# An AdaLN block with sliding-window attention and a mixture of experts: the setup issued in a written order, weight splits on VectorE, and the slot buffer blanked from the load queue

## Chip, cores and metric

The kernel runs on one core of a Trainium2 chip. The metric is the device time of one execution in microseconds, as the median of several runs. A profile is one execution with the hardware profiler on.

## What is computed

Two sequences of 2048 tokens with 256 features go through one block: attention with a window of 128 and 16 heads of 64, then a top-2 mixture of 8 experts with a capacity of 640 rows per expert and choice. Both halves are modulated by rows that come from a small conditioning vector `c` (2 x 256). All is float32. Cut to what matters:

```python
mod = (silu(c) @ wmod).reshape(2, 6, 1, 256)
sa, ca, ga, sb, cb, gb = (mod[:, i] for i in range(6))
ga = sign(ga) * maximum(abs(ga), 0.25)           # gb alike
h = layernorm(x) * (1 + ca) + sa
q, k, v = split(h @ Wqkv)                        # Wqkv 256 x 3072
x = x + ga * (softmax(window(q @ k.T / 8)) @ v) @ Wout   # Wout 1024 x 256
h = layernorm(x) * (1 + cb) + sb
# top-2 of 8 experts per token, 640 rows per expert and choice, later tokens dropped
y = sum over the two choices of prob * (relu(rows @ W1[e] + b1[e]) @ W2[e] + b2[e])
out = x + gb * y
```

## The kernel before

**Precision.** A float32 operand of a large product is split in two parts of type fp32r: the higher, `hi`, is a copy or a scaled copy by ScalarE (ACT), and the lower, `lo`, is the operand less `hi`, by VectorE (DVE) or, for some weights, by GpSimd (POOL). `passes` (L227) makes each product of three matmuls, hi by hi, hi by lo and lo by hi. `split` (L124) splits a loaded weight, `part` (L298) a projection in PSUM.

**Work of the attention.** The 4096 tokens are 16 groups `g` of 256 (two tiles of 128). The 16 heads are 8 pairs. An iteration `w` (L1084) covers two pairs of one group, so there are four iterations to a group, and it works on four stages at once: `new` = the pairs of w (scores, `pack`, `maximum`, first exponentials), `old` = those of w-1 (rest of the exponentials, `normalize`), `turned` = those of w-2 (`turn`, `unpack`, `values`), `done` = those of w-3 (`out_project`). Projections of q and k for iteration w+1 and of v for the group run in the same iteration. `pack` (L510) copies scores from PSUM to SBUF with the window's mask, on ACT (L526) and DVE (L519 for the first group of a sequence, L527). `out_project` uses `wo[:, :, hp, :]`, so pairs 0 to 3 need the first half of Wout (from iteration 3 on) and pairs 4 to 7 the second (from iteration 5 on).

**Order of work.** The attention's iterations stand under `manual_schedule`: each engine runs its instructions in the order in which the program writes them, and so does the queue that SyncE (SP) issues. The setup before it (L322 to L1155) isn't: there a planner orders each engine's instructions by its own estimate. Side work is placed in the iterations by hand: `place` (L1039) puts a generator's steps at given places, such as "1A" (one iteration on, place A), and `go` (L1077) takes one step of each generator that is due at (w, place). `NORM` (L1030) has the places for a group's layer norm, `norm` (L240).

**PSUM.** Six banks are a ring (`bank`, L91) for scores, turned tiles, projections and values; a tile's bank comes free once its reader on ACT or DVE is done.

**Setup.** `norm(0)` makes the first group's normalized rows. The weights of q, k and v come in six pieces of 512 KB (L399 to L407), each loaded by SP to a "raw" buffer and split; the raw buffers are two in the pool `stage` and two in the pool `sp`, taken by turns. POOL does the lower part of three of these pieces and of the second half of Wout. Wout comes in two halves (L409 to L416). The modulation's first two parts are needed as columns (`cols`, L378 to L394), the other four as rows: four rows are made by PE and DVE at L433 to L453 (`wide4`), stored to DRAM (`rowd`, L454) and loaded back broadcast over the partitions (`load_rows`, L116, and `gbr`, L457). `x` is loaded by groups (`load_x`, L203) to three buffers.

**Blanking the slots.** The experts' rows are collected in DRAM in `xbuf`, 10240 rows of 274 floats. Before the first rows are scattered there, each row gets zeros and an invalid token number. The rows' source is the tile `blank`, one row in each partition, in a "raw" buffer of `stage` (L461). `clear(i)` (L465) writes the 1280 rows of an expert with two transfers, each with the row of a partition repeated five times. ACT's queue issues them, four in each of the iterations 1 to 4 (L1088 to L1090).

Of the kernel before, what the change touches and what calls it, by code (L numbers as in the profile page):

```python
# [8 lines left out]
FP = mybir.dt.float32  # L9
FR = mybir.dt.float32r  # L10
I32 = mybir.dt.int32
AF = mybir.ActivationFunctionType
ALU = mybir.AluOpType
# [15 lines left out]
def adaln_block_kernel(  # L29
# [61 lines left out]
    def bank(name, shape=(P, 512)):  # L91
        return ring["pool"].tile(list(shape), FP, tag="ring", name=name, bufs=ring["bufs"])
# [38 lines left out]
            nc.scalar.mul(hi, raw, scale)  # L131
            nc.vector.scalar_tensor_tensor(lo, raw, scale, hi, ALU.mult, ALU.subtract)

    def load(src, shape, name, pool=stage):
        raw = pool.tile(shape, FP, tag="raw", name=f"raw_{name}", bufs=2)
        nc.sync.dma_start(out=raw, in_=src)
        return raw

    def load_split(hi, lo, src, shape, name, scale=None, pool=stage, eng=nc.vector):
        split(hi, lo, load(src, shape, name, pool), scale, eng)  # L140

    class Expert:

# [96 lines left out]
    def norm(g):  # L240

        b = g // GPB
        xg = xs[g]
        mv, rs = norm_stats(xg, f"a{g}")
        yield
        z = wk.tile([P, SBT, D], FP, tag="t2", name=f"z_{g}")
        for t in range(SBT):
            nc.vector.tensor_scalar(
                z[:, t, :], xg[:, t, :], mv[:, t, 0:1], rs[:, t : t + 1],
                ALU.subtract, ALU.mult,  # L250
            )
        yield
        tp = bank(f"tp_h{g}")
        for k in range(ND):
            for t in range(SBT):
                nc.tensor.transpose(
                    tp[:, k * TS + t * P : k * TS + (t + 1) * P], z[:, t, k * P : (k + 1) * P], ident
                )
        hT = wk.tile([P, ND, TS], FP, tag="t2", name=f"hT_{g}")
        for k in range(ND):  # L260
            nc.vector.tensor_scalar(
                hT[:, k, :], tp[:, k * TS : (k + 1) * TS],
                cols[:, 1, k, b : b + 1], cols[:, 0, k, b : b + 1], ALU.mult, ALU.add,
            )
        yield
        hh = wk.tile([P, ND, TS], FR, tag="hh", name=f"hh_{g}")
        hl = wk.tile([P, ND, TS], FR, tag="hl", name=f"hl_{g}")
        nc.scalar.copy(hh, hT)  # L268
        yield
        nc.vector.tensor_tensor(hl, hT, hh, ALU.subtract)  # L270
        hs[g] = (hh, hl)
        yield
# [25 lines left out]
    def part(dh, dl, src):  # L298
        nc.scalar.copy(dh, src)
        nc.vector.tensor_tensor(dl, src, dh, ALU.subtract)  # L300
# [18 lines left out]
        vs[g, t, hf] = v  # L319


    first = norm(0)  # L322
    with tc.tile_pool(name="setup", bufs=1) as sp:
        cr = sp.tile([B * ND, P], FP, name="cr")
# [2 lines left out]
        wm = sp.tile([P, ND, 6 * D], FP, name="wm")  # L327
        wmv = wmod.rearrange("(k p) f -> p k f", p=P)
        nc.sync.dma_start(out=wm[:, :, 0 : 2 * D], in_=wmv[:, :, 0 : 2 * D])
        gw = sp.tile([E, D], FP, name="gw")  # L330
        nc.scalar.dma_start(out=gw, in_=gate_w)
        b1r = sp.tile([E * NF, P], FP, name="b1r")
        nc.scalar.dma_start(out=b1r, in_=b1.rearrange("e (k p) -> (e k) p", p=P))
        nc.scalar.dma_start(
            out=gbias, in_=gate_b.rearrange("(a e) -> a e", a=1).to_broadcast([P, E])
        )
        make_identity(nc, ident)

        nc.gpsimd.memset(ones, 1.0)
# [26 lines left out]
        next(first)  # L366


        sg = sp.tile([B * ND, P], FP, name="sg")
        nc.scalar.activation(sg, cr, AF.Exp, scale=-1.0)  # L370
        nc.vector.tensor_scalar(sg, sg, 1.0, None, ALU.add)
        nc.vector.reciprocal(sg, sg)
        nc.vector.tensor_tensor(sg, sg, cr, ALU.mult)
        tp = bank("tp_c")
        nc.tensor.transpose(tp[:, 0 : B * ND], sg, ident[0 : B * ND, 0 : B * ND])
        scT = sp.tile([P, B, ND], FP, name="scT")
        nc.vector.tensor_copy(scT.rearrange("p b k -> p (b k)"), tp[:, 0 : B * ND])
        mc = bank("mod_cols")  # L378
        for m in range(2):
            for d in range(ND):  # L380
                o = (m * ND + d) * B
                for k in range(ND):
                    nc.tensor.matmul(
                        out=mc[:, o : o + B],
                        lhsT=wm[:, k, m * D + d * P : m * D + (d + 1) * P],
                        rhs=scT[:, :, k],
                        start=(k == 0),
                        stop=(k == ND - 1),
                    )
        colf = cols.rearrange("p m d b -> p (m d b)")  # L390
        nc.vector.tensor_copy(colf[:, 0 : ND * B], mc[:, 0 : ND * B])
        nc.vector.tensor_scalar(
            colf[:, ND * B : 2 * ND * B], mc[:, ND * B : 2 * ND * B], 1.0, None, ALU.add
        )  # L394

        for _ in first:
            pass

        for i in range(2):  # L399
            for j in range(3):  # L400
                f = slice(j * HD + i * HD // 2, j * HD + (i + 1) * HD // 2)
                load_split(
                    wq[:, 0, :, f], wq[:, 1, :, f], wqkv[:, f].rearrange("(k p) f -> p k f", p=P),
                    [P, ND, HD // 2], f"wq{i}_{j}", QSCALE if j == 0 else None,
                    pool=sp if (3 * i + j) % 2 else stage,
                    eng=nc.gpsimd if j == 1 or (i, j) == (0, 2) else nc.vector,
                )  # L407
        nc.sync.dma_start(out=wm[:, :, 2 * D :], in_=wmv[:, :, 2 * D :])
        for i in range(2):  # L409
            s = slice(i * NP // 2, (i + 1) * NP // 2)  # L410
            load_split(
                wo[:, 0, s, :], wo[:, 1, s, :],
                wout[i * HD // 2 : (i + 1) * HD // 2, :].rearrange("(k p) d -> p k d", p=P),
                [P, NP // 2, D], f"wo{i}", pool=stage if i else sp,
                eng=nc.gpsimd if i else nc.vector,
            )  # L416
        part(*project_qk(0, 0, 0))

        tp = bank("tp_g")
        for k in range(ND):  # L420
            nc.tensor.transpose(
# [3 lines left out]
        tp = bank("tp_b1")  # L425
        nc.tensor.transpose(tp[:, 0 : E * NF], b1r, ident[0 : E * NF, 0 : E * NF])
        nc.vector.tensor_copy(b1T, tp[:, 0 : E * NF])


        wide4 = sp.tile([B, 4, D], FP, name="wide4")  # L430
# [2 lines left out]
        for g in range(2):  # L433
            mr = bank(f"mod_rows{g}")
            for k in range(ND):
                nc.tensor.matmul(
                    out=mr[0:B, :],
                    lhsT=scT[:, :, k],
                    rhs=wm[:, k, (2 + 2 * g) * D : (4 + 2 * g) * D],
                    start=(k == 0),  # L440
                    stop=(k == ND - 1),
                )
            gate, plain = (mr[0:B, 0:D], mr[0:B, D:]) if g == 0 else (mr[0:B, D:], mr[0:B, 0:D])
            nc.vector.tensor_scalar(sgn, gate, 0.0, 2.0, ALU.is_ge, ALU.mult)
            nc.vector.tensor_scalar(sgn, sgn, -1.0, None, ALU.add)
            nc.vector.tensor_tensor(mag, gate, sgn, ALU.mult)
            nc.vector.scalar_tensor_tensor(
                wide4[:, 3 * g, :], mag, 0.25, sgn, ALU.max, ALU.mult
            )
            if g == 0:  # L450
                nc.vector.tensor_copy(wide4[:, 1, :], plain)
            else:
                nc.vector.tensor_scalar(wide4[:, 2, :], plain, 1.0, None, ALU.add)  # L453
        nc.sync.dma_start(out=rowd, in_=wide4)  # L454
        load_rows(0)
        for b in range(B):
            nc.sync.dma_start(out=gbr[:, b, :], in_=rowd[b, 3:4, :].to_broadcast([P, D]))  # L457


        xs[1] = load_x(1)  # L460
        blank = stage.tile([P, ROW], FP, tag="raw", name="blank")  # L461
        nc.gpsimd.memset(blank, 0.0)
        nc.gpsimd.memset(blank[:, TOK : TOK + 1].bitcast(I32), 2 * T)

    def clear(i):  # L465

        for r0 in range(i * BUF, (i + 1) * BUF, CAP):
            nc.scalar.dma_start(
                out=xbuf[r0 : r0 + CAP, :].rearrange("(p n) d -> p n d", p=P),
                in_=blank.rearrange("p (a d) -> p a d", a=1).to_broadcast([P, CAP // P, ROW]),  # L470
            )


    wl = attn.enter_context(tc.tile_pool(name="work_late", bufs=2, reuse_waits="tile"))
# [552 lines left out]
    VALUES = [[(0, 0)], [(1, 0)], [(0, 1)], [(1, 1)]]  # L1027
    LAST_VALUES = [[(0, 0), (1, 0)], [(0, 1)], [], []]

    NORM = ["0B", "1A", "1H", "2A", "2B"]  # L1030
    CLOSE = ["0H", "1A", "1B", "2H", "3H", "4A", "4B", "5H", "6A", "6B", "6C"]
    LATE = {
        NG - 3: ["0H", "1A", "1B", "2B", "2H", "3A", "3B", "3H", "3C", "3C", "3C"],
# [49 lines left out]

    def iteration(w):  # L1084
        g, p2 = divmod(w, NP // 2)
        if p2 == NP // 2 - 1 and g + 2 < NG:
            xs[g + 2] = load_x(g + 2)
        for i in range(2 * w - 2, 2 * w):  # L1088
            if 0 <= i < E:
                clear(i)  # L1090
        new, old, turned, done = pair(w), pair(w - 1), pair(w - 2), pair(w - 3)

        ahead = [divmod(i, NP // 2) for i in range(w + 1, NW if w == NW - 3 else w + 2) if i < NW]
# [58 lines left out]
            exps(*new[0], [2, 3])  # L1152
        go(w, "V")

    part(*project_qk(0, 0, 1))  # L1155
    everything = {mybir.EngineType.PE, mybir.EngineType.Activation, mybir.EngineType.DVE, mybir.EngineType.Pool, mybir.EngineType.SP}
    order = tc.manual_schedule(engines=everything)
    order.__enter__()
    for w in range(NW + 3):
        iteration(w)  # L1160

# [135 lines left out]
```

## Time and profile before

| | us |
|---|---|
| median of 3 runs | 1161.58 (1160.19 to 1163.09) |
| the profiled execution | 1161.56 |
| its span, first to last instruction | 1159.8 |

| engine | busy us | share of the span |
|---|---|---|
| PE (matmul) | 1086.3 | 94% |
| PEld (weight load, beside PE) | 999.6 | 86% |
| DVE | 877.4 | 76% |
| ACT | 676.7 | 58% |
| POOL | 593.8 | 51% |

The span's first 30 us or so are the setup, with PE busy 6 tenths of the first slice of 29 us; the attention follows to about 760 us, then the experts. The granted clock of PE is 0.97 on average, with spells of 0.50.

How to read it: a row of a time line has the start, the duration, the engine, the line of the kernel, the operation, what it writes and reads, and in brackets the idle time before it with what ended that. "SPq" and "ACTq" are the queues on which SP and ACT issue transfers; the duration there is that of issuing. "To landing" is the time from issue until the data have arrived. A row for a stretch of time has, for each engine, the busy us in it and the count of instructions, then PE's granted clock, the mean busy share of the 16 DMA engines, and GB/s.

### The profile page before, as it was taken

To read this page: it belongs to the slowest core of one execution; us is meant where nothing else is said; L and a number is where in the kernel's file an instruction comes from. 1 tells how busy PE (TensorE), PEld (TensorE's weight loads), DVE (VectorE), ACT (ScalarE), POOL (GpSimd) and SP (SyncE) were. 2 spreads that over 40 slices of the span, in tenths; PEclk is the share of its full clock that TensorE was granted. 3 is DMA by queue.
4 is the path that set the end of the run, shared out by engine and by line. 5 is a ranking of instruction groups with operands and counts; after the bars stand their busy time and mean duration, and the time that the engine had idled before them with its cause. 6 is when DMAs were issued, how large, how long until landed. Compare 5 with 4: busy or idle time off the path is not lost. (4 is left out here: it accounts for less than half of the span.)

```text
span 1159.8 us, 25187 instructions
## 1 busy us (share of the span) xinstructions
PE 1086.3 (94%) x9246; PEld 999.6 (86%) x9246; DVE 877.4 (76%) x2168; ACT 676.7 (58%) x2097; POOL 593.8 (51%) x769
## 2 busy tenths in 40 slices
PE   6799999999999999999999997779889999999995
PEld 4678999999999888999999896768879999999995
DVE  6556688888878778888878877767667777878764
ACT  4467776777777567777777676423344444344441
POOL 4235465665675556665675665433522615443524
PEclk9899999999999999999999998879989999999998
DMA  6890010010010010010010022233432524342413
GB/s 228 194 218 21 1 39 19 21 39 19 21 39 19 21 43 29 21 36 20 17 37 20 18 65 70 85 91 95 83 106 87 84 84 90 83 89 67 83 45 36
DMA packets 59571, 72.09 MB, mean 62 GB/s; under 512 B 4807, under 2 KB 51152, under 8 KB 59436
## 3 DMA queue, kind: packets, MB, share of 16 engines
q1 hardware_dynamic: 36988, 44.27, 12.2%
q0 software_dynamic: 11712, 14.79, 7.4%
q10 hardware_dynamic: 10736, 11.27, 4.3%
q8 instruction: 80, 1.31, 0.5%
q14 instruction: 55, 0.45, 0.1%
HBM read 40.11 MB, written 32.27 MB: 62 GB/s over the span
## 5 line engine op out<-in xcount | busy, mean ns | idle before, releaser
L937 ACT ACTIVATE hm<-ph,b1T 128x256 fp32r<-128x256 f32 (+2 forms) x184 | 99.3, 540 | 224.8 <-PE ph L232 192.6
L232 PE MATMUL pq<-hh,wq 128*128 128x256 f32 x1024 | 216.8, 295 | 3.5 <-ACT hh L268 3.0
L232 PE MATMUL ph<-xT,we 128*128 128x256 f32 (+2 forms) x1104 | 203.6, 325 | 15.5 <-DVE xT L127 4.6
L550 ACT ACTIVATE pm<-pm,mx 128x128 f32<-128x128 f32 x512 | 204.1, 402 | 19.4 <-DVE mx L536 16.7
L232 PE MATMUL y<-we,hm 128*128 128x256 f32 x1440 | 201.5, 285 | 6.6 <-DVE hm L939 6.6
L232 PEld LDWEIGHTS y<-we,hm 128*128 128x128 f32 x1440 | 186.7, 190 | 10.7 <-DVE hm L939 9.3
L232 PEld LDWEIGHTS ph<-xT,we 128*128 128x128 f32 x1104 | 172.3, 196 | 21.2 <-issue 6.5
L584 POOL TENSOR_SCALAR_AFFINE_SELECT pT<-pT 128x512 f32<-128x512 f32 (+1 forms) x128 | 80.9, 632 | 211.6 <-ACT pT L583 211.5
L232 PEld LDWEIGHTS pq<-hh,wq 128*128 128x128 f32 x1024 | 170.0, 193 | 5.8 <-ACT hh L268 3.4
L938 DVE TENSOR_SCALAR r<-ph,b1T 128x256 f32<-128x256 f32 (+2 forms) x184 | 101.8, 562 | 73.1 <-ACT hm L937 65.6
L560 POOL TENSOR_TENSOR pm<-pm,rd 128x512 f32<-128x512 f32 x128 | 133.8, 1045 | 28.5 <-DVE rd L558 26.4
L232 PE MATMUL pq<-hl,wq 128*128 128x256 f32 x512 | 145.8, 285 | 0.0
L526 ACT COPY pm<-sc 128x256 f32<-128x256 f32 (+1 forms) x256 | 80.6, 363 | 107.9 <-PE sc L502 70.3
L1002 POOL TENSOR_TENSOR ys<-ys,gw 128x256 f32<-128x256 f32 x56 | 48.4, 971 | 175.7 <-DVE ys L992 157.0
L607 PE MATMUL av<-pT,v 128*64 128x128 f32 (+1 forms) x1472 | 126.7, 321 | 4.7 <-POOL pT L588 2.2
L607 PEld LDWEIGHTS av<-pT,v 128*64 128x64 f32 x1472 | 91.1, 140 | 33.7 <-POOL pT L588 4.6
L1003 POOL DMA_INDIRECT out_dram<-ys,tok x60 | 98.1, 1634 | 33.5 <-issue 11.4
L527 DVE COPY_PREDICATED pm<-within,sc 128x256 f32<-128x256 int32 (+1 forms) x256 | 96.1, 422 | 22.0 <-ACT pm L526 21.1
L502 PE MATMUL sc<-kr,qh 64*128 64x256 f32 (+1 forms) x1024 | 105.7, 296 | 5.0 <-DVE ql L300 2.0
L550 ACT ACTIVATION_READ_ACCUMULATOR pm<-pm,mx 128x1 f32 x512 | 99.6, 194 | 0.0
L232 PEld LDWEIGHTS pq<-hl,wq 128*128 128x128 f32 x512 | 99.0, 193 | 0.0
L939 DVE TENSOR_TENSOR hm<-r,hm 128x256 fp32r<-128x256 f32 (+2 forms) x144 | 94.6, 657 | 5.3
(162 smaller groups left out, 2261.9 us busy)
## 6 DMA issues: line engine op xcount, KB each, us to landing
raw_w<-in_L_ffn_W_dram SPq DMA_DIRECT2D x32, 512.0 KB, 3.9
xbuf<-blank ACTq DMA_DIRECT2D x16, 685.0 KB, 9.6
xt<-xbuf SPq DMA_DIRECT2D x8, 822.0 KB, 4.9
x<-in_L_attn_x_dram SPq DMA_DIRECT2D x16, 256.0 KB, 2.8
out_dram<-x SPq DMA_DIRECT2D x16, 256.0 KB, 2.3
xt<-xbuf SPq DMA_DIRECT2D x7, 548.0 KB, 5.0
raw_wq<-in_L_attn_Wqkv_dram SPq DMA_DIRECT2D x6, 512.0 KB, 7.0
wm<-in_L_wmod_dram SPq DMA_DIRECT2D x1, 1024.0 KB, 11.1
```

The costliest lines, as they stand in the source:

```text
L232: nc.tensor.matmul(out=out_, lhsT=a, rhs=b, start=start and n == 0 and i == 0, stop=stop and n == last and i == 2, **kw,)
L502: nc.tensor.matmul(out=sc[h][:, t, lo:], lhsT=q[r, t * P : (t + 1) * P], rhs=kr[r, (0, 1, 0)[i], hp, blk, :], start=(i == 0), stop=(i == 2),)
L526: nc.scalar.copy(pm[:, h, ts, :], blocks[:, own, :])
L527: nc.vector.copy_predicated(pm[:, h, ts, :], within.rearrange("p (a k) -> p a k", a=1).to_broadcast([P, n, P]), blocks[:, before, :],)
L550: nc.scalar.activation(pm[:, h, t, :], pm[:, h, t, :], AF.Exp, bias=mx[:, h, t : t + 1], accum_out=den[:, h, t : t + 1],)
L560: nc.gpsimd.tensor_tensor(pmv, pmv, rd.rearrange("p h (t a) -> p (h t) a", a=1).to_broadcast([P, 2 * SBT, P]), ALU.mult,)
L584: nc.gpsimd.affine_select(out=pT[:, :, t0:, 0, :], in_=own[:, :, t0:, :], pattern=[[0, 2], [0, n], [-1, P]], compare_op=ALU.is_gt, fill=0. ...
L607: nc.tensor.matmul(out=av[h * DH : (h + 1) * DH, q0 : q0 + hi - lo], lhsT=v[:, f0 + h * DH : f0 + (h + 1) * DH], rhs=pT[:, h, lo:hi], star ...
L937: nc.scalar.activation(hh[:, s], phv, AF.Relu, bias=bias)
L938: nc.vector.tensor_scalar(r[:, s], phv, bias, 0.0, ALU.add, ALU.max)
L939: nc.vector.tensor_tensor(hl, r[:, 0:W], hh, ALU.subtract)
L1003: add = nc.gpsimd.indirect_dma_start(out=of, out_offset=bass.IndirectOffsetOnAxis(ap=tok[:, 0:1], axis=0), in_=y, in_offset=None, bounds_c ...
```

## The change

- `manual_schedule` is entered ahead of the setup, so that the setup too runs in written order on all five engines. The setup's text is put in another order for it.
- The six weight pieces of q, k and v get five raw buffers in `sp`, and functions of their own: `get(n)` loads, `high(n)` is ACT's part, `low(n)` DVE's. POOL has no lower part any more; `load_split` is gone. Pieces 0 to 2 are loaded ahead of the small loads of `gw`, `b1` and the gate's bias, which move from ACT's queue to SP's; then the rest of `wmod`, `x` of group 1, pieces 3 and 4. Piece 5 is loaded after the first two projections.
- The layer norm has one more step (between the transposes and `hT`); `NORM` has "1H" twice for it.
- `norm(0)`'s steps, the splits, the two first projections, the gate's and bias's transposes and the modulation rows are interleaved by hand. The modulation rows come after both first projections.
- `blank` is filled early. `clear` has no argument: it issues all sixteen transfers, on SP's queue, once, before iteration 0.
- Wout is loaded by a generator, `load_output`: its first step (before the loop) loads the first half, its second (iteration 1, place A) splits that half and loads the second, its third (iteration 1, place C) splits the second.
- `x` of group 2 is loaded before the loop; it stood in iteration 3, and the planner issued it at about 6 us.

```diff
-    def load_split(hi, lo, src, shape, name, scale=None, pool=stage, eng=nc.vector):
-        split(hi, lo, load(src, shape, name, pool), scale, eng)
...
+    everything = {
+        mybir.EngineType.PE, mybir.EngineType.Activation, mybir.EngineType.DVE,
+        mybir.EngineType.Pool, mybir.EngineType.SP,
+    }
+    order = tc.manual_schedule(engines=everything)
+    order.__enter__()
     first = norm(0)
...
+        def get(n):
+            raws[n] = load(
+                wqkv[:, columns(n)].rearrange("(k p) f -> p k f", p=P), [P, ND, HD // 2],
+                f"wq{n}", sp, 5,
+            )
+
+        def high(n):
+            if n % 3:
+                nc.scalar.copy(wq[:, 0, :, columns(n)], raws[n])
+            else:
+                nc.scalar.mul(wq[:, 0, :, columns(n)], raws[n], QSCALE)
+
+        def low(n):
+            hi, lo = (wq[:, m, :, columns(n)] for m in range(2))
+            if n % 3:
+                nc.vector.tensor_tensor(lo, raws[n], hi, ALU.subtract)
+            else:
+                nc.vector.scalar_tensor_tensor(lo, raws[n], QSCALE, hi, ALU.mult, ALU.subtract)
+
+        for n in range(3):
+            get(n)
         gw = sp.tile([E, D], FP, name="gw")
-        nc.scalar.dma_start(out=gw, in_=gate_w)
+        nc.sync.dma_start(out=gw, in_=gate_w)
...
+        nc.sync.dma_start(out=wm[:, :, 2 * D :], in_=wmv[:, :, 2 * D :])
+        xs[1] = load_x(1)
+        for n in range(3, 5):
+            get(n)
...
+        blank = stage.tile([P, ROW], FP, tag="raw", name="blank", bufs=2)
...
+        high(0)
+        low(0)
         colf = cols.rearrange("p m d b -> p (m d b)")
...
+        next(first)
+        high(1)
         for _ in first:
             pass
...
+        low(1)
+        high(2)
         part(*project_qk(0, 0, 0))
-
+        low(2)
+        high(3)
+        part(*project_qk(0, 0, 1))
+        get(5)
         tp = bank("tp_g")
...
         nc.vector.tensor_copy(b1T, tp[:, 0 : E * NF])
+        low(3)
+        high(4)
+        low(4)
+        high(5)
...
+        low(5)
         nc.sync.dma_start(out=rowd, in_=wide4)
         load_rows(0)
         for b in range(B):
             nc.sync.dma_start(out=gbr[:, b, :], in_=rowd[b, 3:4, :].to_broadcast([P, D]))
...
-    def clear(i):
-
-        for r0 in range(i * BUF, (i + 1) * BUF, CAP):
-            nc.scalar.dma_start(
+    def clear():
+
+        for r0 in range(0, NSLOT, CAP):
+            nc.sync.dma_start(
                 out=xbuf[r0 : r0 + CAP, :].rearrange("(p n) d -> p n d", p=P),
                 in_=blank.rearrange("p (a d) -> p a d", a=1).to_broadcast([P, CAP // P, ROW]),
             )
+
+    def load_output():
+
+        for i in range(2):
+            s = slice(i * NP // 2, (i + 1) * NP // 2)
+            raw = load(
+                wout[i * HD // 2 : (i + 1) * HD // 2, :].rearrange("(k p) d -> p k d", p=P),
+                [P, NP // 2, D], f"wo{i}",
+            )
+            yield
+            split(wo[:, 0, s, :], wo[:, 1, s, :], raw)
...
-    NORM = ["0B", "1A", "1H", "2A", "2B"]
+    NORM = ["0B", "1A", "1H", "1H", "2A", "2B"]
...
-        if p2 == NP // 2 - 1 and g + 2 < NG:
+        if p2 == NP // 2 - 1 and g and g + 2 < NG:
             xs[g + 2] = load_x(g + 2)
-        for i in range(2 * w - 2, 2 * w):
-            if 0 <= i < E:
-                clear(i)
...
-    part(*project_qk(0, 0, 1))
-    everything = {mybir.EngineType.PE, mybir.EngineType.Activation, mybir.EngineType.DVE, mybir.EngineType.Pool, mybir.EngineType.SP}
-    order = tc.manual_schedule(engines=everything)
-    order.__enter__()
+    outputs = load_output()
+    next(outputs)
+    xs[2] = load_x(2)
+    clear()
+    place(outputs, 1, ["0A", "0C"])
     for w in range(NW + 3):
         iteration(w)
```

More of the change, by code (lines that the diff above doesn't have):

```diff
@@ L132, in split, with load @@
             nc.vector.scalar_tensor_tensor(lo, raw, scale, hi, ALU.mult, ALU.subtract)
-    def load(src, shape, name, pool=stage):
-        raw = pool.tile(shape, FP, tag="raw", name=f"raw_{name}", bufs=2)
+    def load(src, shape, name, pool=stage, bufs=2):
+        raw = pool.tile(shape, FP, tag="raw", name=f"raw_{name}", bufs=bufs)
         nc.sync.dma_start(out=raw, in_=src)
         return raw
-    def load_split(hi, lo, src, shape, name, scale=None, pool=stage, eng=nc.vector):
-        split(hi, lo, load(src, shape, name, pool), scale, eng)
     class Expert:
@@ L329, in adaln_block_kernel, with columns @@
         nc.sync.dma_start(out=wm[:, :, 0 : 2 * D], in_=wmv[:, :, 0 : 2 * D])
+        def columns(n):
+            i, j = divmod(n, 3)
+            return slice(j * HD + i * HD // 2, j * HD + (i + 1) * HD // 2)
+        raws = {}
+        def get(n):
[16 more added lines that the diff above has]
+            get(n)
         gw = sp.tile([E, D], FP, name="gw")
-        nc.scalar.dma_start(out=gw, in_=gate_w)
+        nc.sync.dma_start(out=gw, in_=gate_w)
         b1r = sp.tile([E * NF, P], FP, name="b1r")
-        nc.scalar.dma_start(out=b1r, in_=b1.rearrange("e (k p) -> (e k) p", p=P))
-        nc.scalar.dma_start(
+        nc.sync.dma_start(out=b1r, in_=b1.rearrange("e (k p) -> (e k) p", p=P))
+        nc.sync.dma_start(
             out=gbias, in_=gate_b.rearrange("(a e) -> a e", a=1).to_broadcast([P, E])
         )
+        nc.sync.dma_start(out=wm[:, :, 2 * D :], in_=wmv[:, :, 2 * D :])
+        xs[1] = load_x(1)
+        for n in range(3, 5):
+            get(n)
         make_identity(nc, ident)
@@ L366, in adaln_block_kernel @@
         next(first)
+        blank = stage.tile([P, ROW], FP, tag="raw", name="blank", bufs=2)
+        nc.gpsimd.memset(blank, 0.0)
+        nc.gpsimd.memset(blank[:, TOK : TOK + 1].bitcast(I32), 2 * T)
         sg = sp.tile([B * ND, P], FP, name="sg")
@@ L377, in adaln_block_kernel @@
         nc.vector.tensor_copy(scT.rearrange("p b k -> p (b k)"), tp[:, 0 : B * ND])
+        next(first)
         mc = bank("mod_cols")
@@ L394, in adaln_block_kernel @@
         )
+        next(first)
+        high(1)
         for _ in first:
             pass
[L399 to L416, printed above, removed]
+        low(1)
+        high(2)
         part(*project_qk(0, 0, 0))
+        low(2)
+        high(3)
+        part(*project_qk(0, 0, 1))
+        get(5)
         tp = bank("tp_g")
@@ L457, in adaln_block_kernel @@
             nc.sync.dma_start(out=gbr[:, b, :], in_=rowd[b, 3:4, :].to_broadcast([P, D]))
[L460 to L463, printed above, removed]
-    def clear(i):
-        for r0 in range(i * BUF, (i + 1) * BUF, CAP):
-            nc.scalar.dma_start(
+    def clear():
+        for r0 in range(0, NSLOT, CAP):
+            nc.sync.dma_start(
                 out=xbuf[r0 : r0 + CAP, :].rearrange("(p n) d -> p n d", p=P),
@@ L471, in clear @@
             )
+    def load_output():
[5 more added lines that the diff above has]
+            )
+            yield
+            split(wo[:, 0, s, :], wo[:, 1, s, :], raw)
     wl = attn.enter_context(tc.tile_pool(name="work_late", bufs=2, reuse_waits="tile"))
```

## The prediction, made before the changed kernel was run

> **What bounds the kernel now.** I read the page first, then the busy time by stretches of 5 and 10 us, then the time lines of ACT, SP, DVE and POOL over the first 95 us, and last the landings of single transfers. The chain that ended last is of no help here: it holds only the last 4 us, indirect writes by POOL. The stretches show where the changed part matters (engine busy us, granted clock, DMA share, GB/s):
>
> ```profile
> 35.00:40.00 5.00, 2.25 (x12) 1.44 (x10) 3.32 (x9) 2.08 (x10) 1.11 (x1) 0.98 0.67 194
> 40.00:45.00 5.00, 3.83 (x26) 2.99 (x24) 2.66 (x6) 3.18 (x12) 1.04 (x1) 0.50 1.11 236
> ...
> 90.00:100.00 10.00, 10.00 (x95) 9.02 (x94) 6.13 (x14) 7.23 (x26) 3.33 (x5) 1.00 0.00 1
> ```
>
> From 85 us on PE is busy 10.00 of 10 us at full clock, and with few gaps up to about 660 us: what comes there is bound by PE, so whatever the changed first 85 us gain or lose arrives at the end almost one to one. Before 85 us PE has holes and spells at half clock. I use as milestones the first instruction of `pack` (L519, or L526 from iteration 4 on) of iterations w = 0 to 5: 32.66, 44.59, 57.14, 69.20, 81.89, 92.85 us. What stretches them is on ACT:
>
> ```profile
> 48.13 0.52 ACTq L468 DMA_DIRECT2D xbuf<-blank  x1
> 49.03 0.52 ACTq L468 DMA_DIRECT2D xbuf<-blank  x1
> ...
> 49.59 1.27 ACTq L468 DMA_DIRECT2D xbuf<-blank  x1
> ...
> 50.90 1.47 ACTq L468 DMA_DIRECT2D xbuf<-blank  x1
> 52.41 0.59 ACT L583 COPY pT<-tp 128x512 f32<-128x512 f32 x1 [2.50 <-issue]
> ```
>
> ACT has finished its exponentials at 49.9, but the next copy starts only behind the fourth transfer that ACT issues. It loses about 2.5 us here, 1.9 at w=3 and 2.9 at w=4. The other fact is the size of these transfers:
>
> ```profile
> xbuf<-blank ACTq DMA_DIRECT2D x16, 685.0 KB, 9.6
> ```
>
> Sixteen of 685 KB are 11.2 MB. While they run, the DMA share is 1.1 and the rate about 235 GB/s, so the DMA engines are full; the whole takes about 48 us, from 36.2 to 86. The profile's queue table says the same: 4.3% of 16 engines' span, 50 us. I take 49 us, 3.07 us each.
>
> Third, SP's queue lands in order. SP issued 1 MB of `wm`, and just behind it two loads of x, 256 KB each (second fence: the landing of x, issue to landing):
>
> ```profile
> 4.55 0.48 SPq L408 DMA_DIRECT2D wm<-in_L_wmod_dram  x1
> 5.07 1.80 SPq L205 DMA_DIRECT2D x<-in_L_attn_x_dram  x2
> ```
>
> ```profile
> DMA to landing us min/median/max: 2.9/11.2/11.3
> ```
>
> The first x, with only 2 KB ahead of it, took 2.9 us; these took 11.2, landing at 16.3, just behind `wm` (4.55 + 11.1 = 15.65).
>
> Fourth, DVE is slowed by POOL's halves of the weight splits:
>
> ```profile
> 14.21 3.08 DVE L132 SCALAR_TENSOR_TENSOR wq<-raw_wq,wq 128x1024 fp32r<-128x1024 f32 x1 [1.44 <-ACT wq L131]
> ...
> 19.91 2.26 DVE L445 TENSOR_SCALAR sgn<-sgn 2x256 f32<-2x256 f32 x1
> ```
>
> The same L132 takes 1.23 us alone, and L445's neighbours 0.4; both long ones end when a POOL L127 does (one ran 19.65 to 22.03).
>
> **What the Trainium skill says.** DMA: Bandwidth & Descriptors, "Queues, rings and completion order": SP and ACT own one ring each on the same 16 engines, and each engine consumes a ring in order. The x landings agree. The same page, "Issuing engines are not separate DMA queues": a move between issuers saves only the sequencer's time. Agreed as far as shown: what ACT loses is issue time, while the 48 us are the engines'. GPSIMD Engine Reference, "Specifications": POOL shares its SBUF interfaces with VectorE; the 3.08 against 1.23 us agree. TensorE: Matmul & The Clock Gate, "Part 1": PE falls to half clock after an idle window of some 3.4 us. Here it fell at 39.8, behind the hole from 36.5, and stayed there 10.2 us.
>
> **Part by part.**
>
> *Lower parts on DVE, fixed order.* Removed from POOL: three subtractions of 2.3 to 2.4 us for `wq`, one of 3.7 for `wo`. Added to DVE: 4 x 1.21 us, but DVE loses the stretched instructions (1.9 at L132, about 1.9 and 2.1 at L445). The loads keep their pace: `wq0` to `wq2` land at 9.0, 10.4, 11.8, the rest of `wm` at about 14.5, x1 15.3, `wq3` 16.6, `wq4` 18.0, `wq5` 19.4 (512 KB per 1.35 us). Three small loads move from ACT to SP, ahead of `wm`: three issues of 0.6 us at the start, hidden behind transfers. Following DVE's new list: low(0) ends 11.4, hT 13.3, hl 14.7, low(1) 15.9, ql 17.0, low(2) 18.2, low half of kr 19.0, two copies 19.3, low(3) 20.5, low(4) 21.7. Then the modulation rows, five instructions at a pitch of 0.34 us for each of two halves: 25.2 (PE's rows, 5.3 us behind the second projection, are ready by 23.2). low(5) ends 26.3. So `wide4` is stored at 25.2 instead of 30.5, and iteration 0 packs at about 28.9 instead of 32.7 (two lower halves of 0.67 and the statistics, 1.2, come first): 3.8 us gained.
>
> *ACT's sixteen issues removed.* ACT gets back 2.5 + 1.9 + 2.9 us, and about 2.5 at w=1. With those out, the pitch of `pack` is 10.05, 10.1, 9.85 for w=1 to 4; 10.96 stays for w=4 to 5.
>
> *Queue order on SP.* This is the step that decides. SP now issues: rows' store (25.2), rows (26.6, since it waits for the store, 1.38 us in the profile), two `gbr` (to 27.9), the first half of Wout (28.3), x2, then all sixteen blanking transfers from 29.3, and only in iteration 1 the second half of Wout. Rows and gbr land at 31.2, Wout's half 1.35 later, x2 at 33.2. The blanking fills the ring from there: 33.2 + 49 = 82.3. Wout's second half lies behind it in the ring and lands at 82.3 + 1.4 = 83.7. If it must also wait for the buffer that `blank` holds (both have the tag "raw" with two buffers, and the profile doesn't show which is given), it is issued at 82.4 and lands 4.2 us later (raw_wo's landing), 86.6. I take the middle, 85.2.
>
> *The wait added.* The generator's third step, the split of that half, is placed in iteration 1 at "C", ahead of iteration 1's `pack`. ACT reaches it at about 39 us. Queued behind it on ACT: the pack copies, exponentials, unpack, qh and kr. On DVE its subtraction stands ahead of L519. PE can still do iteration 1's scores (1.9 us), one turn (0.5) and one projection (1.5); then all six banks of the ring are held by tiles that ACT has not read, and PE stops, for some 40 us. Nothing needs this half before `out_project` of iteration 5: the cover is missing only because the place is early. ACT's copy takes 1.05, DVE's subtraction 1.2: iteration 1 packs at 85.2 + 2.25 = 87.4.
>
> *After the wait.* To iteration 5's `pack`: 10.05 + 10.1 + 9.85 + 10.96 = 41 us. PE is about 4 us of work ahead, but comes out of a long hole: 3.4 to 10.2 us at half clock cost 0 to 5 us (half of the spell, less the lead). I take 2. So iteration 5 packs at 87.4 + 41 + 2 = 130.4 instead of 92.85: 37.5 us later. From there the work is the same and PE is the bound. The profiled execution took 1161.56 (span 1159.8 and 1.8 around it; the median of the runs is 1161.58): 1161.6 + 37.5 = **1199 us**.
>
> The ends of what is unknown: iteration 1 packs 1.4 us earlier or later by the buffer, the blanking begins up to 3 us earlier or later (DVE's list is an estimate), and half clock gives -2 to +3. All together, 1199 - 6.4 = 1192.6 to 1199 + 7.4 = 1206.4.
>
> **Rivals.** *The second half of Wout is not late.* If it overtook the blanking, the two gains would stand alone: iteration 1 packs at 28.9 + 11 = 40 (pitch 9.5 without ACT's issues, plus 1.5 for the two splits), iteration 5 at 81, 12 us earlier: 1149.5. The place is SP's ring; the point from which it decides is a landing at 49.6 us (92.85 - 41 - 2.25), where the two kernels tie. For it speaks only that the trace has no load queued behind a blanking transfer on one ring; against it the x loads, and 11.2 MB that would have to pass in 16 us, 700 GB/s, where the busiest stretch here moves 400. Chance 0.09. *Late, but half-hidden*: PE and POOL have work from other iterations to fill the hole. The banks speak against it; with 10 us filled it would be 1189. Chance 0.06. *Later still*: blanking starts only at the old time of the rows, 5.3 us later, or two iterations run at half clock, 5 more: 1204 to 1209. Chance 0.14. My forecast's case: 0.69. Two per cent are left for a tie.
>
> **How the numbers follow.** The slower cases hold 0.89; a measurement of this kernel can tell 0.3%, 3.5 us, from no change. The range 1189 to 1208 takes in the unknown ends, most of the later case and the edge of the half-hidden one, and leaves out the fast rival and about 0.1 beside. Faster 0.09, same 0.02, slower 0.89.
>
> **What would show it.** Right: all blanking on SP's queue from about 29 us, DMA share 1.1 to about 82; Wout's second half landing at 84 to 87; one ACT wait on that load of about 45 us in iteration 1, a PE hole of the same stretch, then pitches of about 10 us. The gain steps: `wide4` stored near 25, no L132 or L445 over 1.3 us. Wrong: no ACT wait at that copy, or a blanking that ends much before 80 us.

## The result and the profile after

The changed kernel takes 1197.21 us (median of 4 runs, 1195.06 to 1198.80) against 1162.34 (the three runs of the table above and one more, 1160.19 to 1163.36): a ratio of 1.0299, with a 95% interval of 1.0276 to 1.0321. It is slower by 3%, 35 us. The profiled execution took 1198.8 us, with a span of 1197.0.

The lines below answer to those shown of the kernel before. First the busy time by stretches (PE, weight load, DVE, ACT, POOL, then granted clock, DMA share, GB/s):

```profile
35.00:40.00 5.00, 3.03 (x17) 2.25 (x17) 3.98 (x8) 4.57 (x16) 1.76 (x2) 0.62 1.10 292
40.00:45.00 5.00, 4.93 (x27) 4.70 (x27) 1.17 (x3) 0.02 (x1) 0.40 (x1) 0.50 1.12 241
45.00:50.00 5.00, 0.32 (x2) 0.02 (x1) 0.00 (x0) 0.00 (x0) 0.00 (x0) 0.50 1.11 231
50.00:60.00 10.00, 0.00 (x0) 0.00 (x0) 0.00 (x0) 0.00 (x0) 0.00 (x0) 0.50 1.12 237
...
80.00:85.00 5.00, 0.00 (x0) 0.00 (x0) 0.00 (x0) 0.00 (x0) 0.00 (x0) 0.50 0.94 195
85.00:90.00 5.00, 0.00 (x0) 0.00 (x0) 1.44 (x3) 1.31 (x2) 0.00 (x0) 0.50 0.04 14
```

From 45.3 to 87 us no compute engine does anything. Before it stops, PE has done iteration 1's scores, one turn and one projection, which is the work that the prediction left to it. Until 80 us the DMA engines are full (share 1.1, the blanking). The time line from 86 us shows what ends the hole:

```profile
87.15 1.04 ACT L127 CAST wo<-raw_wo 128x1024 fp32r<-128x1024 f32 x1 [47.13 <-DMA raw_wo<-in_L_attn_Wout_dram]
88.23 1.22 DVE L127 TENSOR_TENSOR wo<-raw_wo,wo 128x1024 fp32r<-128x1024 f32 x1 [47.06 <-ACT wo L127]
89.37 0.28 DVE L562 TENSOR_TENSOR pm<-sc,after 128x128 f32<-128x128 f32 x1
...
90.43 1.09 PE L617 MATMUL tp<-ident,pm 128*128 128x128 f32 x4 [45.11 <-DVE pm L570]
```

ACT had waited 47.1 us for the second half of Wout, with DVE behind it, and iteration 1 packs only at 89.4 us. PE had waited 45.1 us for a bank that the pack frees. SP's queue (issue and its duration) shows why the half came then:

```profile
29.73 0.43 SPq L136 DMA_DIRECT2D raw_wo<-in_L_attn_Wout_dram  x1
30.21 0.51 SPq L202 DMA_DIRECT2D x<-in_L_attn_x_dram  x1
30.82 42.08 SPq L500 DMA_DIRECT2D xbuf<-blank  x16
72.99 2.54 SPq L136 DMA_DIRECT2D raw_wo<-in_L_attn_Wout_dram  x1
```

It was issued at 73.0, right behind the sixteenth blanking transfer, and landed 14.1 us later, at 87.1:

```profile
DMA to landing us min/median/max: 6.2/10.2/14.1
```

(The shortest is the first half's.) From 100 to 660 us PE is busy 9.9 of 10 us on average, so the delay goes through to the end.

### The profile page after: what moved, and what is told of

The parts are those of the page before. It is cut to its first block, busy times and chain, and to the rows that moved or that the text cites. A ratio compares the mean times of both kernels' runs of the same rounds, so it can differ in the third digit from the quotient of the medians.

```text
span 1197.0 us, 25182 instructions
## 1 busy us (share of the span) xinstructions
PE 1083.4 (91%) x9246; PEld 1000.3 (84%) x9246; DVE 875.9 (73%) x2172; ACT 676.1 (56%) x2097; POOL 582.6 (49%) x765
## 3 DMA queue, kind: packets, MB, share of 16 engines
q1 hardware_dynamic: 47724, 55.54, 16.4%
## 5 line engine op out<-in xcount | busy, mean ns | idle before, releaser
L229 PEld LDWEIGHTS y<-we,hm 128*128 128x128 f32 x1440 | 186.9, 190 | 10.5 <-DVE hm L982 9.1
L650 PE MATMUL av<-pT,v 128*64 128x128 f32 (+1 forms) x1472 | 124.3, 317 | 5.1 <-POOL pT L631 2.2
L617 PE MATMUL tp<-ident,pm 128*128 128x128 f32 x512 | 81.7, 285 | 47.7 <-DVE pm L570 47.7
L1046 POOL DMA_INDIRECT out_dram<-ys,tok x60 | 98.3, 1638 | 29.8 <-issue 11.0
L617 PEld LDWEIGHTS tp<-ident,pm 128*128 128x128 f32 x512 | 57.7, 143 | 59.5 <-issue 48.7
L545 PE MATMUL sc<-kr,qh 64*128 64x256 f32 (+1 forms) x1024 | 103.2, 294 | 1.3 <-DVE ql L298 0.8
## 6 DMA issues: line engine op xcount, KB each, us to landing
xbuf<-blank SPq DMA_DIRECT2D x16, 685.0 KB, 16.4
```

The source lines that it names most:

```text
L229: nc.tensor.matmul(out=out_, lhsT=a, rhs=b, start=start and n == 0 and i == 0, stop=stop and n == last and i == 2, **kw,)
L545: nc.tensor.matmul(out=sc[h][:, t, lo:], lhsT=q[r, t * P : (t + 1) * P], rhs=kr[r, (0, 1, 0)[i], hp, blk, :], start=(i == 0), stop=(i == 2),)
L617: nc.tensor.transpose(tp[:, h, t, :], pm[:, h, t, :], ident)
L650: nc.tensor.matmul(out=av[h * DH : (h + 1) * DH, q0 : q0 + hi - lo], lhsT=v[:, f0 + h * DH : f0 + (h + 1) * DH], rhs=pT[:, h, lo:hi], star ...
L1046: add = nc.gpsimd.indirect_dma_start(out=of, out_offset=bass.IndirectOffsetOnAxis(ap=tok[:, 0:1], axis=0), in_=y, in_offset=None, bounds_c ...
```

## The experiments

All are compared with runs of the kernel before on the same chip. "Iteration n packs" is the first instruction of `pack` in it, as in the prediction.

**Both halves of Wout first.** `load_output` issues both loads before the loop, ahead of the blanking; the row to be copied moves to another buffer.

```diff
-        blank = stage.tile([P, ROW], FP, tag="raw", name="blank", bufs=2)
+        blank = cl.tile([P, 1, ROW], FP, tag="xt", name="blank", bufs=1)[:, 0, :]
...
+        raws = [
+            load(
+                wout[i * HD // 2 : (i + 1) * HD // 2, :].rearrange("(k p) d -> p k d", p=P),
+                [P, NP // 2, D], f"wo{i}",
+            )
+            for i in range(2)
+        ]
+        yield
         for i in range(2):
             s = slice(i * NP // 2, (i + 1) * NP // 2)
-            raw = load(
-                wout[i * HD // 2 : (i + 1) * HD // 2, :].rearrange("(k p) d -> p k d", p=P),
-                [P, NP // 2, D], f"wo{i}",
-            )
+            split(wo[:, 0, s, :], wo[:, 1, s, :], raws[i])
             yield
-            split(wo[:, 0, s, :], wo[:, 1, s, :], raw)
```

> The changed kernel with both halves of Wout loaded ahead of the sixteen blanking transfers (the row that they copy lies in another buffer). If the loss is the place of the second half of Wout in SP's queue, ACT's wait of 47 us goes and both gains stand alone: iteration 1 packs at about 42 instead of 89.4, so 1197 - 47 = 1150 us. If the loss comes from blanking that competes with the attention for memory or engines, the time stays at 1190 or more.

Measured: 1152.97 us (6 runs), ratio 0.9904 [0.9889, 0.9920]. Both splits in iteration 1 on ACT's time line:

```profile
36.30 1.05 ACT L127 CAST wo<-raw_wo 128x1024 fp32r<-128x1024 f32 x1 [0.94 <-DMA raw_wo<-in_L_attn_Wout_dram]
...
40.23 1.05 ACT L127 CAST wo<-raw_wo 128x1024 fp32r<-128x1024 f32 x1
```

The second waits for nothing, and iteration 1 packs at 42.5. While the attention runs, the blanking goes on at a share of 1.1 up to 80 us:

```profile
60.00:70.00 10.00, 10.00 (x94) 8.97 (x93) 5.67 (x16) 6.38 (x27) 3.48 (x6) 1.00 1.13 248
70.00:80.00 10.00, 10.00 (x93) 8.96 (x92) 7.54 (x20) 9.73 (x36) 7.17 (x12) 1.00 1.10 254
```

PE is busy 10.00 of 10 us beside it. So the loss is not the blanking as such, which decides between the two theories of the expectation. This edit changes the order of the loads and the buffer of the copied row together; the next experiment separates them.

**The second half on ACT's queue.** Only this load changes its ring; SP blanks as before. So that its place among the blanking is real, twelve of the transfers copy a second row, which POOL fills in iteration 1.

```diff
-                [P, NP // 2, D], f"wo{i}",
+                [P, NP // 2, D], f"wo{i}", queue=nc.scalar if i else nc.sync,
             )
+            if i:
+                blank2 = cl.tile([P, 1, ROW], FP, tag="xt", name="blank2", bufs=1)[:, 0, :]
+                nc.gpsimd.memset(blank2, 0.0)
+                nc.gpsimd.memset(blank2[:, TOK : TOK + 1].bitcast(I32), 2 * T)
+                clear(blank2, 4 * CAP, NSLOT)
             yield
...
-    clear()
+    clear(blank, 0, 4 * CAP)
```

> The changed kernel with the second half of Wout loaded from ACT's queue in iteration 1, while SP's queue still blanks (4 transfers before the loop, 12 from iteration 1, with a second row as their source). If the order within SP's ring makes the load late, this one, on the other ring, lands within some 7 us of its issue at about 38.5, ACT waits about 3 us, and the time is about 1155. If the full DMA engines make it late whatever the ring, it lands near 85 and the time stays near 1197.

Measured: 1161.5 us (20 runs), ratio 0.9977 [0.9968, 0.9985].

```profile
38.58 0.41 ACTq L136 DMA_DIRECT2D raw_wo<-in_L_attn_Wout_dram  x1
39.04 0.40 ACT L598 ACTIVATE pm<-pm,mx 128x128 f32<-128x128 f32 x1 [1.75 <-DVE wo L127]
...
49.07 1.04 ACT L127 CAST wo<-raw_wo 128x1024 fp32r<-128x1024 f32 x1 [6.95 <-DMA raw_wo<-in_L_attn_Wout_dram]
```

The load takes 10.5 us beside the blanking and ACT waits 7 us, not 47. So the place behind the blanking in SP's queue makes it late, not the full engines. It isn't the buffer either: `blank` lies where it lay, and ACT issues the load when DVE has split the first half (the wait of 1.75 us), so what the load needs is the first half's buffer.

The sizes were off. Iteration 1 packs at 51.3, 8.8 us later than in the first experiment: 7 us are the wait for the load, and nearly 2 are ACT's wait until it can issue it. PE is at half clock until 55 us, but that costs nothing more: from iteration 1 to 5 it is 40.6 us here and 40.7 there.

**The split later.** The load stays behind the blanking; the third step of the generator moves from iteration 1 to iteration 4.

```diff
-    place(outputs, 1, ["0A", "0C"])
+    place(outputs, 1, ["0A", "3C"])
```

> The changed kernel with only the split of the second half moved from iteration 1 to iteration 4, place C; the load stays behind the blanking and still lands near 87. If the place of the waiting instruction sets the loss, iterations 1 to 3 pass at a pitch of 10 us, ACT comes to the split at about 70 and waits some 16 us instead of 47: 1197 - 30 = 1167. If the load itself or the blanking holds the engines, the time stays near 1197.

Measured: 1166.18 us (20 runs), ratio 1.0021 [1.0011, 1.0030].

```profile
82.60 1.04 ACT L127 CAST wo<-raw_wo 128x1024 fp32r<-128x1024 f32 x1 [12.02 <-DMA raw_wo<-in_L_attn_Wout_dram]
```

Iterations 1 to 3 pack at 40.8, 50.7, 60.7; ACT then waits 12.0 us. The place of the waiting instruction alone is worth 31 us. The two pitches, 9.9 and 10.0 us, lie beside the blanking; the changed kernel has the same two, 9.9 and 10.0, after its blanking is over.

**Blanking twice.**

```diff
-        for r0 in range(0, NSLOT, CAP):
+        for r0 in [*range(0, NSLOT, CAP)] * 2:
             nc.sync.dma_start(
```

> The changed kernel with each of the sixteen blanking transfers issued twice (the values are the same). If the wait lasts as long as the blanking, sixteen more at 3.07 us add 49 us to it: 1197 + 49 = 1246, and ACT waits about 96 us. If something else holds the second half of Wout, the time changes little.

Measured: 1237.93 us (4 runs), ratio 1.0637 [1.0614, 1.0659].

```profile
126.44 1.04 ACT L127 CAST wo<-raw_wo 128x1024 fp32r<-128x1024 f32 x1 [86.48 <-DMA raw_wo<-in_L_attn_Wout_dram]
```

The wait grows with the blanking, from 47.1 to 86.5 us, by 39.4, and the time by 40.7. It is less than the 49 expected, because the transfers run faster in this kernel's profile: the packets of 32 take 90.4 us, 2.8 each, where those of sixteen take 51.0, 3.2 each, in the changed kernel's.

**The kernel before, with only the blanking moved to SP.**

```diff
-        for i in range(2 * w - 2, 2 * w):
-            if 0 <= i < E:
-                clear(i)
...
     order.__enter__()
+    clear()
```

(`clear` is the changed kernel's.)

> The kernel before with one part of the change alone: all sixteen blanking transfers on SP's queue ahead of the loop, none on ACT's (both halves of Wout are loaded in the setup there, ahead of the blanking). If what ACT loses is the time to issue the transfers (2.5, 2.5, 1.9 and 2.9 us), the four iterations shorten by that and the time is about 1153. If the blanking hurts by filling the DMA engines, it stays at 1162. The planner puts x of group 2 and the modulation rows behind the blanking; if they come late, a wait on them in iterations 4 to 6 shows it, with up to some us lost.

Measured: 1154.66 us (7 runs), ratio 0.9935 [0.9916, 0.9955], 8.2 us less. Iterations 1 to 3 pack at 41.1, 51.0 and 61.2, a pitch of 10 us as in the changed kernel. So taking the issues off ACT is worth 8 us by itself. Two things come with the edit: the planner issues the blanking from 22.6 us on, ahead of the rows' store, and iteration 0 packs 0.9 us earlier, for a reason that is open. The rows' loads are issued behind the blanking (at 60.9), and no wait on them shows; `x` of group 2 (issued at 58.1) does come late:

```profile
71.55 0.43 DVE L219 BATCH_NORM_STATS2 st_a<-x 128x6 f32<-128x256 f32 x1 [2.35 <-DMA x<-in_L_attn_x_dram]
```

The step from iteration 4 to 5, in which this wait lies, takes 11.5 us.

**The changed kernel with the blanking back on ACT.**

```diff
-    clear()
...
+        for i in range(2 * w - 2, 2 * w):
+            if 0 <= i < E:
+                clear(i)
```

> The changed kernel with the blanking back on ACT's queue, four transfers in each of iterations 1 to 4: the setup in the written order alone. The second half of Wout, on the other ring, shares the engines with four transfers and lands about 10 us after its issue. By the prediction's step for the setup, iteration 0 packs 2 to 4 us earlier than in the kernel before; ACT then waits a few us in iteration 1: 1158 to 1162. If the second half of Wout were late for another reason than SP's ring, it would stay near 1197.

Measured: 1168.27 us (4 runs), ratio 1.0048 [1.0030, 1.0066]: slower than the kernel before, where 1158 to 1162 was expected.

```profile
48.85 1.04 ACT L127 CAST wo<-raw_wo 128x1024 fp32r<-128x1024 f32 x1 [7.20 <-DMA raw_wo<-in_L_attn_Wout_dram]
```

Iteration 0 packs at 29.8, 2.9 us before the old 32.7. But iteration 1 now holds both splits of Wout (1.7 us each, by the step from 40.8 to 42.5 between the third and the first experiment) and this wait of 7.2 us, and packs at 51.1 instead of 44.6. The 47 us are gone here as well, with the blanking on the other ring. From iteration 0 to 1 it takes 9.3 us more than in the kernel before, three times what the written setup gains; the splits and the wait at their place, 3.4 and 7.2 us, account for that.

**POOL's lower parts again.** The kernel with both halves first, and `low(1)`, `low(2)`, `low(4)` on POOL.

```diff
-                nc.vector.tensor_tensor(lo, raws[n], hi, ALU.subtract)
+                eng = nc.gpsimd if n in (1, 2, 4) else nc.vector
+                eng.tensor_tensor(lo, raws[n], hi, ALU.subtract)
```

> The kernel with both halves of Wout first (1153), and the lower parts of pieces 1, 2 and 4 on POOL as in the kernel before. If POOL's subtractions (2.3 us against 1.2 on DVE) and the stretched DVE instructions beside them cost what the prediction said, iteration 0 packs 1 to 4 us later: 1154 to 1157. If they are hidden, 1153.

Measured: 1152.79 us (4 runs), ratio 0.9914 [0.9897, 0.9930], no different from 1152.97. DVE and POOL in the setup:

```profile
21.91 2.01 DVE L483 TENSOR_SCALAR sgn<-sgn 2x256 f32<-2x256 f32 x1
```

```profile
20.50 3.27 POOL L358 TENSOR_TENSOR wq<-raw_wq,wq 128x1024 fp32r<-128x1024 f32 x1 [3.69 <-ACT wq L350]
```

The stretched instruction is back (2.01 us, 0.28 for its twin), but DVE has three subtractions fewer; iteration 0 packs at 30.3 against 30.1. In this setup the move from POOL to DVE is worth nothing.

**Both halves first, splits late.** A version that the runs pointed to: as the first experiment, with the splits placed where PE is nearly the bound.

```diff
-    place(outputs, 1, ["0A", "0C"])
+    place(outputs, 1, ["1S", "2S"])
```

> The kernel with both halves of Wout first, and the two splits moved from iteration 1 to iterations 2 and 3, behind the pack, where PE is the bound or nearly. Each split in iteration 1 costs 1.7 us on the path of ACT and DVE (iteration 1 packs at 40.8 with one, 42.5 with two). If both are hidden in their new places: 1153 - 3.5 = 1149.5. If iteration 2 or 3 has no room either: 1153.

Measured: 1150.94 us (4 runs), ratio 0.9900 [0.9881, 0.9919]. Iteration 1 packs at 39.0 instead of 42.5. It is the fastest median of the study, 1.0% below the kernel before; its interval overlaps that of the version with the splits in iteration 1, which ran on another chip, so that the last 2 us are likely, not shown.

## Why the prediction was right, step by step

| step | predicted us | profile |
|---|---|---|
| `wide4` stored | 25.2 | 27.0 |
| iteration 0 packs | 28.9 | 30.3 |
| blanking issued from | 29.3 | 30.8 |
| ACT reaches the split | 39 | 40.0 |
| second half of Wout lands | 85.2 (83.7 to 86.6) | 87.1 |
| iteration 1 packs | 87.4 | 89.4 |
| four pitches, half clock | 41 + 2 | 39.8 + 0 |
| iteration 5 packs | 130.4 | 129.2 |
| later than before, here | 37.5 | 36.4 |
| time | 1199 | 1198.8 profiled, 1197.2 median |

- **What decides** was right, cause and size. The first experiment removes the loss by the order of SP's loads (with the row's buffer), the second by the queue with the row's buffer as it was, the third most of it by the place of the split alone, and the fourth nearly doubles the wait with the length of the blanking. The rival on the other side, 1149.5 us with the half in time, came out at 1153.0 once the half was in time: iteration 1 packed at 42.5, where its sum had 40, since the two splits take 1.7 us each, not 1.5 together, and iteration 0 packed 1.2 us later than predicted. The prediction quotes that a move between issuers saves only the sequencer's time. Here that time was large: SP took 42.1 us to issue the sixteen transfers.
- **How near the total is, is partly luck.** Iteration 1 packs 2.0 us later than predicted, and the four pitches with the half clock take 3.2 us less; the two errors nearly cancel.
- **The buffer.** The half was issued while earlier blanking transfers were still under way (they land 16.4 us after issue in the median), so it did not wait for `blank`'s buffer. This is the earlier of my two cases, 83.7. It landed at 87.1 because the blanking began about 1.5 us later than estimated and ran a little slower: its packets run from 34.3 to 85.2, 51 us, 3.2 each, not 3.07. The prediction's "about 48 us, from 36.2 to 86" was a slip: between these times lie 49.8 us, near the 49 that it went on with.
- **The setup** was mis-sized: 2.4 us gained at iteration 0, not 3.8. The step that failed is "ql 17.0, low half of kr 19.0". I gave each projection 1.5 us, at full clock. In the setup they ran at little over half that pace, one matmul every 0.21 us, where from 23.3 us on it is one every 0.12:

```profile
14.98 0.41 PE L229 MATMUL pq<-hl,wq 128*128 128x256 f32 x1
```

Later in the trace the same matmul takes 0.28 us. The half of kr ended at 20.7, and what lies behind it on DVE came 1.4 to 1.8 us later. The stretches print a clock of 1.00 there, so that only the matmuls' own durations show it.
- **Lower parts on DVE.** That L132 and L445 (L359 and L482 in the changed kernel) lose their stretch was right:

```profile
9.73 1.23 DVE L359 SCALAR_TENSOR_TENSOR wq<-raw_wq,wq 128x1024 fp32r<-128x1024 f32 x1 [2.38 <-ACT wq L352]
...
23.57 0.28 DVE L482 TENSOR_SCALAR sgn<-sgn 2x256 f32<-2x256 f32 x1
```

That this gains anything was not: with POOL's parts back the time is the same. The 2.4 us gained at iteration 0 come from the rest of the written setup; which part of it gives them was not tried.
- **ACT's issues.** 2.5 + 2.5 + 1.9 + 2.9, 9.8 us. With this edit alone the steps from iteration 0 to 4 shorten by about that, from 49.2 to 39.3 us, and 8.2 us of it arrive in the time. In the changed kernel the pitches of 9.93, 10.00 and 9.71 are those predicted (10.05, 10.1, 9.85); the fourth is 10.20, where I had kept 10.96 from a stretch that had begun at half clock.
- **Half clock behind the hole.** I took 2 us. PE restarted at 90.4 at half pace and was at full clock by 95, and its lead covered it: iteration 2 packs 9.93 us after iteration 1. Nothing lost. The second experiment agrees: its spell of half clock, from 38 to 55 us, began ahead of the long hole, ended 2.8 us after PE's restart at 52.3, and cost nothing at the packs. The hole from 36.5 that the prediction names was not idle throughout: in the 3.4 us ahead of the fall at 39.8 PE worked 0.65 us, and its longest idle stretch was 2.1 us, less than the idle window of 3.4 us that the prediction quotes.
- **The median** lies 1.6 us below the profiled execution; the other three runs are at 1195.1 to 1198.5. A blanking whose pace moves from one execution to the next would do this. The profiles show different paces only between different kernels, one execution of each, so the reason is open.

## What to carry to other kernels

A queue that is moved must be read to its end: what a load costs depends on the bytes ahead of it in the same ring, so 512 KB behind 11 MB landed 50 us later than ahead of it (87.1 against 36.7 us), though no engine needed the 11 MB then. In a fixed order the first instruction that waits for such a load stops everything behind it on its engine. So put the load ahead of the bulk, and the instruction that waits late, near its first use, where another engine is the bound. An engine that only issues transfers still pays for them: with ACT's sixteen issues gone the kernel took 8 us less.

## What the runs showed of the hardware that I had not expected

- The same blanking, by the same sixteen transfers, took 51.0 us in the changed kernel's profile (222 to 241 GB/s in most stretches) and 45.9 in that of the first experiment (232 to 265). What sets the pace is open; in the experiment with twice the transfers it made 40 us of 49.
- A 512 KB load on ACT's ring took 10.5 us beside a full SP ring (8.9 in the kernel with the rings exchanged), against 4.2 in the setup before and 14.1 behind the blanking in SP's own ring, where it could also be issued only at 73.0. A second ring is not free, but it doesn't wait for the first one's queue.
- With the DMA engines full for 45 us (share 1.1), the attention kept its pace: 9.9 and 10.0 us from pack to pack in the third experiment, as without them.
